# Where a soft threshold keeps its magnitudes: PSUM or SBUF, and two PSUM banks that change hands

## The chip, the core and the metric

The kernel runs on one core of a Trainium2 chip. TensorE (PE) multiplies, VectorE (DVE), ScalarE (ACT) and GpSimd (POOL) work element by element, and SyncE (SP) issues the transfers. Every engine runs its own instructions in the order of the program and waits on semaphores. Two memories lie beside the engines: SBUF, and PSUM, into which PE writes. PSUM is used here as eight banks; one bank holds 512 float32 numbers for each of the 128 partitions. The metric is the time of the program on the device in microseconds (us), and less is better.

## The reference

The input `x` is 4 images of 64 channels of 256 x 256 float32. Four layers follow each other:

```python
# layers 0, 2, 3: a 2-D convolution by FFT, zero padded to 512 x 512,
# with a separable filter per channel (hx, hy come out of two small networks)
k = jnp.einsum('ijk,imk->ijmk', hx, hy)[0]
y = irfft2(rfft2(x, s=(512, 512)) * rfft2(k) / 512)[..., :256, :256]
out = y + x * bias[:, None, None]
# layer 1: 2-D Haar transform, mixing of channels, soft threshold, inverse
f1 = haar2d(x)
for i in range(2):
    f4 = jnp.einsum('bchw,oc->bohw', f1 * v[i], conv_w[i])
    acc = acc + jnp.sign(f4) * jax.nn.relu(jnp.abs(f4) - tau[i])
y = haar2d(acc, inverse=True) + x
```

## The kernel before

All data are float32. The filter is separable, so a convolution is two products with Toeplitz matrices, rows and then columns. The images are taken in two **groups** of two images; each group goes through 32 rounds of two channels. The function `toeplitz` (L289) issues one block of a product: 16 products of 64 x 64 tiles with 256, 192, 128 and 64 columns, which the profile shows as 32 matmuls. `haar` (L302) issues a block of the Haar transform, 8 matmuls of 512 columns in the profile.

There are three phases, and each is a list of small pieces of program that `beside` (L929) lays among each other. The order on every engine is therefore written out by hand; no scheduler moves anything.

- Phase A (`phase_a`): layer 0 and the forward Haar transform, for both groups, into a DRAM tensor.
- Phase B (`phase_b(grp)`): the mixing of channels and the soft threshold. `phase_b(0)` lies beside the second half of phase A, and `phase_b(1)` beside the first half of phase C.
- Phase C (`phase_c`): the inverse Haar transform, then layers 2 and 3. For rounds t of group 0 it runs beside `phase_b(1)`; after that, from `beside(c[cut_c:], [], 0, 0)` on, it runs alone.

**Phase B.** It goes through 64 steps s of two units, u = 2s and u = 2s+1, one for each of the two sums over `i`. Of each unit:

- `mix` (L597): PE multiplies by `conv_w` into `f4`, a tile of two PSUM banks, of which there is one (`bufs=1`). 8 matmuls of 512 columns.
- `multiply` (L616, L622): DVE, `x = f4 * v`, from PSUM into SBUF. Two buffers.
- `sign` (L624, L628): ACT, `m = Sign(x)`, into SBUF. Three buffers.
- `magnitude` (L630, L634): ACT, `a = Abs(x)`, into `a`, a tile of two PSUM banks, one buffer.
- `less` (L636, L639): DVE, `a = a - tau`, in place.
- `threshold` (L641, L644): DVE, `m = max(a, 0) * m`, into SBUF.
- `add` (L652): POOL adds `m` and the old value into `g` (L659, L662, L663), and `store` (L666) issues the transfer to DRAM.

In the second group the odd units of steps 2 to 63 are **raw**: `multiply` only copies `f4` to SBUF (L619), and their threshold is done in phase C, when that runs alone (`shrink`, L761, with its operations at L778 to L787). So the second group has 66 units that take a magnitude (128 less 62 raw ones). Each of them brings one `less` and one `threshold`.

The pieces of `phase_b` are emitted in this order (L678): in piece j=0 of unit u come `multiply(u)`, `less(u-1)`, `add(u-2)`; in j=1 `mix(u+1)`, `sign(u)`, `threshold(u-1)`; in j=2 `magnitude(u)`. DVE therefore reads, step after step: multiply of 2s, copy of raw 2s+1, less of 2s, threshold of 2s, with the instructions of phase C between them.

**Phase C.** A round t has 18 pieces (L869): four blocks of rows of layer 2 (`c1r`), one of the inverse transform (`c0ps`), four of columns of layer 3 of round t-2 (`c2c`), four of rows of layer 3 of round t-1 (`c2r`), one `c0ps`, four of columns of layer 2 (`c1c`). Two blocks in a row share a pair of PSUM banks; a `c0ps` block has a pair of its own. A pair is emptied by two copies, which are emitted at the head of the next piece (`flush`): ACT copies `c1r`, `c2r` (L836) and `c0ps` (L824), and DVE adds the bias term to `c1c` and `c2c` (L855). POOL does the free part of the inverse transform (`ci`, L382), and its result is what `c0ps` multiplies.

**Who has which banks.** `banks` (L132) hands out pairs from a list of pools, `rings`, in turn. While phase C runs beside `phase_b(1)`, `rings` is `[acps]`, a pool of four banks, so two pairs take turns; the other four banks are `f4` and `a`. When phase C runs alone, `a` and `f4` are free: two banks become a third pair (`wide2`), and two hold the late threshold (`late_ps`).

```python
def banks(name):
    ring = rings[asked[0] % len(rings)]
    asked[0] += 1
    return [ring.tile([P, 2, N], F32, tag="ps", name=f"{name}_{r}") for r in range(2)]
```

Of the kernel before, what the change touches and what calls it, by code (L numbers as in the profile page):

```python
# [41 lines left out]
F32 = mybir.dt.float32  # L42
AF = mybir.ActivationFunctionType
ALU = mybir.AluOpType
PSUM = bass.MemoryType.PSUM
DRAM = bass.MemoryType.DRAM

P = 128
# [17 lines left out]
GROUPS = 2  # L66
NB = B // GROUPS
# [12 lines left out]
W = 2 * N  # L80
# [16 lines left out]
def conv_haar_kernel(  # L97
# [18 lines left out]
    def pool(name, bufs, stack=ctx, **kw):  # L116
        return stack.enter_context(tc.tile_pool(name=name, bufs=bufs, reuse_waits="tile", **kw))

    ac = pool("ac", 2)
    acps = pool("acps", 4, space=PSUM)  # L120
# [8 lines left out]
    rings = [acps]  # L129
# [391 lines left out]
    def phase_b(grp):  # L521
# [4 lines left out]
        def raw(u):  # L526
            return grp == GROUPS - 1 and u % 2 == 1 and FULL <= u // 2 < STEPS
        st = [dict() for _ in range(STEPS)]
        un = [dict() for _ in range(units)]
# [100 lines left out]
        def magnitude(u):  # L630
            if raw(u):
                return
            un[u]["a"] = bps.tile([P, NB, W], F32, tag="a", name=f"a_{grp}_{u}", bufs=1)
            nc.scalar.activation(un[u]["a"], un[u]["x"], AF.Abs)  # L634

        def less(u):  # L636
# [41 lines left out]
        def piece(u, j):  # L678
# [17 lines left out]
            elif j == 1:  # L696
                if u + 1 < units:
                    mix(u + 1)
                if u < units:
                    sign(u)  # L700
                if i and s < STEPS and grp == GROUPS - 1:
                    store_raw(s)
                if 0 < u <= units:
                    threshold(u - 1)
                if i == 0 and s > 0:

                    load_v(s + 2)
                    load_f(s + 3)
            else:
                if u < units:  # L710
                    magnitude(u)
                if i == 0 and s < STEPS:
                    exchange(s)
# [237 lines left out]
    bps = pool("bps", 2, during, space=PSUM)  # L951
# [3 lines left out]
    a, head = a[-2 * A_PIECES :], A_PIECES + BLOCKS  # L955
# [2 lines left out]
    beside(a_last, c_before[5:], 0, 5)  # L958
    during.close()
    bp = pool("b2", 2, during)  # L960
    bps = pool("bps2", 2, during, space=PSUM)

    mid = 3 * BLOCKS + 2
    main = c_first + a_end[:1] + c[:BLOCKS] + c[mid:C_PIECES] + a_end[1:] + c[BLOCKS:mid] + c[C_PIECES:cut_c]
    beside(main, phase_b(1), len(c_first) + len(a_end) + 2 * BLOCKS, 0)
    during.close()
    rings[:] = [acps, acps, pool("wide2", 2, space=PSUM)]
    late["sb"] = pool("late", 1)
    late["ps"] = pool("late_ps", 1, space=PSUM)
    beside(c[cut_c:], [], 0, 0)  # L970
# [119 lines left out]
```

## Time and profile before

| | |
|---|---|
| three runs | 2595.73, 2596.64, 2599.01 us; median 2596.64 |
| the profiled execution | 2597.8 us; its span 2595.7 us, so 2.1 us lie around the span |
| mean granted clock of TensorE | 0.979 |
| busy, share of the span | PE 2343.0 us (90%), DVE 1800.2 (69%), ACT 1325.6 (51%), POOL 2025.0 (78%) |
| moved by DMA | 685.25 MB, mean 264 GB/s |
| `phase_b(1)` beside phase C | first `multiply` at 1166.9 us, last `threshold` at 1880.8 us |

A row of the group view names line, engine, operation, output and inputs, the number of instructions, their busy time and mean duration, and the idle time of the engine before them with what ended it. In a timeline a row is: start in us, length in us, engine, line, operation, and in square brackets the time that the engine had waited and what released it. In a row of stretches the columns are the stretch, its length, and the busy time of PE, PEld (TensorE's weight loads), DVE, ACT and POOL, the granted clock, the busy share of the DMA engines and their GB/s.

### The profile page before, as it was taken

The page shows a single profiled execution, that of the slowest core. Times are in us where ns is not written, and L with a number is a line of the kernel's source. Part 1 is how long each engine was busy: PE and PEld are TensorE (multiplying, and loading weights), DVE is VectorE, ACT ScalarE, POOL GpSimd, SP SyncE. Part 2 cuts the span into 40 slices and gives each one's busy share as a digit, 9 for nine tenths or more (in the row PEclk, how much of TensorE's full clock was granted, in tenths as well). Part 3 has the DMA queues.
Part 4 walks back from the last instruction along what each step waited for, and adds up shares of the span by engine and source line. Part 5 has one row for each costly group of instructions (what it writes and reads, how often), then busy time and mean ns, then how long its engine had stood idle before and what let it go on. Part 6 is the DMA issues. An engine that isn't in the chain of part 4 may idle for free.

```text
span 2595.7 us, 118630 instructions
## 1 busy us (share of the span) xinstructions
PE 2343.0 (90%) x53292; PEld 1915.7 (74%) x53292; DVE 1800.2 (69%) x2049; ACT 1325.6 (51%) x2187; POOL 2025.0 (78%) x2428
## 2 busy tenths in 40 slices
PE   5999999788888888768999999999989999999999
PEld 4887877444444444547777877788889999999998
DVE  2555445799999999646666666666658777777773
ACT  1221112566666666226666665666655655655552
POOL 1898887899999999757657666766679999999991
PEclk8999999899999999979999999999999999999999
DMA  7676897699999999556989888888776666666653
GB/s 209 222 242 231 289 311 281 245 347 317 343 330 328 347 319 335 180 194 214 333 302 315 317 303 302 306 304 311 275 224 203 220 208 215 214 220 207 220 165 113
DMA packets 203678, 685.25 MB, mean 264 GB/s; under 512 B 29289, under 2 KB 30826, under 8 KB 190755
## 3 DMA queue, kind: packets, MB, share of 16 engines
q1 hardware_dynamic: 203171, 677.67, 75.8%
q8 instruction: 418, 6.85, 1.1%
q14 instruction: 89, 0.73, 0.1%
HBM read 427.93 MB, written 249.63 MB: 261 GB/s over the span
## 4 chain that ended last, share of the span: by engine, by line
PE 59%; DVE 13%; DMA 8%; POOL 8%; issue 5%; ACT 3%; SPq 2%; DVEq 0%; ACTq 0%; POOLq 0%
PE c2c L293 10%; PE c2r L293 9%; PE c1c L293 9%; PE c1r L293 9%; PE a1ps L293 6%; PE a2ps L293 5%; PE f L603 4%; PE c0ps L305 4%; DMA v<-in_v 3%; DVE x L622 3%; POOL fw L341 3%; POOL f L343 2%; DVE a L639 2%; DVE m L644 2%; PE a3ps L305 2%
## 5 line engine op out<-in xcount | busy, mean ns | idle before, releaser
L293 PEld LDWEIGHTS a2ps<-toep,ay 64*64 64x64 f32 x8192 | 313.2, 138 | 161.7 <-DVE f L474 85.0
L382 POOL TENSOR_TENSOR i<-i,g 128x16 f32<-128x16 f32 x744 | 398.3, 556 | 27.7 <-ACT g L359 0.6
L293 PE MATMUL a2ps<-toep,ay 64*64 64x128 f32 (+3 forms) x8192 | 360.1, 307 | 50.8 <-DVE f L474 42.4
L603 PE MATMUL f<-ft,mix 64*64 64x512 f32 x2048 | 312.0, 619 | 95.6 <-DVE x L622 80.2
L293 PEld LDWEIGHTS c2c<-toep,ch 64*64 64x64 f32 x8192 | 314.6, 134 | 59.0 <-ACT ch L836 25.9
L293 PEld LDWEIGHTS a1ps<-toep,x 64*64 64x64 f32 x8192 | 293.8, 134 | 83.8 <-issue 43.1
L293 PE MATMUL a1ps<-toep,x 64*64 64x64 f32 (+3 forms) x8192 | 338.8, 300 | 15.3 <-issue 12.3
L293 PEld LDWEIGHTS c1c<-toep,ch 64*64 64x64 f32 x8192 | 313.3, 134 | 51.6 <-ACT ch L836 26.6
L662 POOL TENSOR_TENSOR gt<-m,ft 128x512 f32<-128x512 f32 x128 | 163.6, 1278 | 236.3 <-DVE m L644 230.7
L293 PE MATMUL c1r<-toep,z 64*64 64x128 f32 (+3 forms) x8192 | 324.4, 299 | 21.5 <-issue 11.6
L293 PE MATMUL c2c<-toep,ch 64*64 64x192 f32 (+3 forms) x8192 | 328.7, 300 | 11.8 <-ACT ch L836 8.7
L293 PEld LDWEIGHTS c1r<-toep,z 64*64 64x64 f32 x8192 | 303.9, 134 | 46.6 <-issue 22.2
L293 PE MATMUL c1c<-toep,ch 64*64 64x128 f32 (+3 forms) x8192 | 324.3, 299 | 11.1 <-ACT ch L836 10.4
L382 POOL TENSOR_TENSOR ci<-i,g 128x1024 f32<-128x1024 f32 x124 | 318.2, 2586 | 4.5
L293 PE MATMUL c2r<-toep,cy 64*64 64x128 f32 (+3 forms) x8192 | 318.4, 298 | 2.9 <-issue 2.7
L293 PEld LDWEIGHTS c2r<-toep,cy 64*64 64x64 f32 x8192 | 301.4, 134 | 24.7 <-issue 13.3
L441 ACT COPY ay<-a1ps 128x512 f32<-128x512 f32 x256 | 137.4, 589 | 353.6 <-PE a1ps L293 353.0
L628 ACT ACTIVATE m<-x 128x1024 f32<-128x1024 f32 x194 | 206.3, 1063 | 194.2 <-DVE x L622 87.6
L639 DVE TENSOR_TENSOR a<-a,v 128x1024 f32<-128x1024 f32 x192 | 236.3, 1231 | 49.0 <-ACT a L634 48.9
L836 ACT COPY ch<-c2r 128x512 f32<-128x512 f32 x256 | 137.5, 591 | 247.1 <-PE c2r L293 246.6
L634 ACT ACTIVATE a<-x 128x1024 f32<-128x1024 f32 x194 | 199.6, 1029 | 109.4 <-DVE m L644 109.4
L855 DVE SCALAR_TENSOR_TENSOR cy<-z,bias_sb,c1c 128x512 f32<-128x512 f32 x256 | 176.9, 742 | 109.5 <-PE c1c L293 109.5
(80 smaller groups left out, 3869.2 us busy)
## 6 DMA issues: line engine op xcount, KB each, us to landing
toep<-filt SPq DMA_DIRECT2D x384, 224.0 KB, 5.3
ft<-coef SPq DMA_DIRECT2D x128, 512.0 KB, 7.4
v<-in_v SPq DMA_DIRECT2D x64, 1024.0 KB, 9.4
mixed<-gt SPq DMA_DIRECT2D x128, 512.0 KB, 7.5
g<-mixed SPq DMA_DIRECT2D x256, 256.0 KB, 5.7
x<-in_x SPq DMA_DIRECT2D x128, 256.0 KB, 4.7
coef<-f SPq DMA_DIRECT2D x128, 256.0 KB, 4.2
x<-in_x SPq DMA_DIRECT2D x32, 1024.0 KB, 7.8
```

The lines of the kernel that those rows point to most:

```text
L293: nc.tensor.matmul(ps[r][half(c), j % 2, k * ROW :], data[half(r), c, k, bass.ts(j, ROW)], t(r, c)[:, : N - k * ROW], start=k == 0, stop=k ...
L305: nc.tensor.matmul(ps[r][half(c)].rearrange("p h k -> p (h k)"), matrix[half(r)], pairs(r, c).rearrange("p h k -> p (h k)"), start=True, s ...
L341: nc.gpsimd.tensor_tensor(diffs, even, odd, ALU.subtract)
L382: engine.tensor_tensor(to, s, d, op)
L441: later(lambda y=y, ps=ps: nc.scalar.copy(y, ps))
L603: nc.tensor.matmul(un[u]["f4"][half(q), b, :], mixers[0][half(r), bass.ts(i, C)], st[s]["f"][half(r), b], start=True, stop=True, tile_posi ...
L628: nc.scalar.activation(un[u]["m"], un[u]["x"], AF.Sign)
L634: nc.scalar.activation(un[u]["a"], un[u]["x"], AF.Abs)
L639: nc.vector.tensor_tensor(un[u]["a"], un[u]["a"], both(u, "tau"), ALU.subtract)
L662: nc.gpsimd.tensor_tensor(g[:, 0], m[:, 0], st[s]["f"][:, 0], ALU.add)
L836: later(lambda y=y, ps=ps: nc.scalar.copy(y, ps))
L855: nc.vector.scalar_tensor_tensor(to, of, bias_sb[:, at : at + 1], ps, ALU.mult, ALU.add)
```

## The change

In the second group `magnitude` no longer takes the PSUM tile `a`: it writes |x| over `x` in SBUF, and `less` and `threshold` work from there. The two banks that `a` had are handed to `rings` as a third pair already while phase C runs beside `phase_b(1)`, and not only when it runs alone. The first group keeps `a` in PSUM.

```diff
         def magnitude(u):
             if raw(u):
                 return
-            un[u]["a"] = bps.tile([P, NB, W], F32, tag="a", name=f"a_{grp}_{u}", bufs=1)
+            if grp == GROUPS - 1:
+                un[u]["a"] = un[u]["x"]
+            else:
+                un[u]["a"] = bps.tile([P, NB, W], F32, tag="a", name=f"a_{grp}_{u}", bufs=1)
             nc.scalar.activation(un[u]["a"], un[u]["x"], AF.Abs)
...
     bp = pool("b2", 2, during)
+    rings[:] = [acps, acps, pool("wide2", 2, space=PSUM)]
     bps = pool("bps2", 2, during, space=PSUM)
...
     during.close()
-    rings[:] = [acps, acps, pool("wide2", 2, space=PSUM)]
     late["sb"] = pool("late", 1)
```

The instructions of every engine and their order are the same before and after; only the places of the operands and the waits differ. Because three lines are added, lines from 634 on carry a number three higher in the profile after (four higher between the two places of `rings`).

## Prediction

> **What bounds the kernel now.** I read the busy time by stretches first: phase C beside `phase_b(1)` (1170 to 1890 us), and phase C alone (1960 to 2500).
>
> ```profile
> 1170.00:1890.00 720.00, 677.89 (x15469) 567.18 (x15465) 453.67 (x477) 448.06 (x786) 482.14 (x571) 1.00 0.85 298
> 1960.00:2500.00 540.00, 539.26 (x14729) 512.86 (x14725) 417.65 (x446) 315.45 (x587) 504.57 (x504) 1.00 0.66 213
> ```
>
> PE leads in both. Alone, it is full; beside the mixing it has gaps, while DVE, ACT and POOL are idle a third of the time. To size the gaps I put the matmuls of the timeline in order of start. Where nothing holds PE, a Toeplitz block of 32 matmuls starts 1.09 us after the one before, a block of 8 (`f`, `c0ps`) takes 0.86 us. From the first to the last whole block of the first stretch 719.5 us pass, and its blocks at these paces make 633.1: PE stalls for 86.4 us. Alone, with three pairs of banks, it is 5.7 us of 537.8.
>
> Then I asked what ended each of the stalls over 0.1 us: the DVE or ACT instruction that ended within 0.15 us before PE went on. Three kinds come out.
>
> (1) **Bank stalls**, 18.5 us. The block needs a pair of banks whose emptying copy has just ended (0.05 us before); 21 blocks, 14.8 us, and in 17 of them the second half waits 0.2 us more for the second copy, 3.7 us. Nearly all are the block behind a `c0ps`: `c0ps` takes only 0.86 us, and the pair used before it is wanted again. The waits of the weight loads name them, and the timeline shows one.
>
> ```profile
> PEld c1c L293 <- ACT ch L836: 19.4, 29, 2.1
> PEld c2c L293 <- ACT ch L836: 16.9, 31, 1.9
> ```
>
> ```profile
> 1520.36 1.07 PE L305 MATMUL c0ps<-ci,inverse_sb 64*64 64x512 f32 x6
> ...
> 1520.51 1.25 ACT L650 COPY other<-ft 64x512 f32<-64x512 f32 x2
> ...
> 1521.78 1.07 ACT L836 COPY ch<-c2r 128x512 f32<-128x512 f32 x2
> ...
> 1522.42 2.66 PE L293 MATMUL c1c<-toep,ch 64*64 64x256 f32 x58 [0.99 <-ACT ch L836]
> ```
>
> ACT was at `other` when `c2r` was done; the first of the two copies (0.6 us each) ended at 1522.37, and PE went on at 1522.42.
>
> (2) **Stalls at the mixing**, 17.3 us in 21 places: `mix(u+1)` needs the only `f4`, and DVE has not read unit u out of it. Below, DVE must add `o` first, which PE itself releases, and `multiply` ends at 1310.39.
>
> ```profile
> 1307.85 1.41 DVE L855 SCALAR_TENSOR_TENSOR o<-cy,bias_sb,c2c 128x512 f32<-128x512 f32 x2 [1.00 <-PE c2c L293]
> ...
> 1309.17 1.22 DVE L622 TENSOR_TENSOR x<-f,v 128x1024 f32<-128x1024 f32 x1
> ...
> 1310.53 1.09 PE L603 MATMUL f<-ft,mix 64*64 64x512 f32 x8 [0.48 <-DVE x L622]
> ```
>
> (3) The rest, some 50 us: no data wait ends it ("issue"), or `ci` was late once (5.5 us at 1219).
>
> **The change, part by part.** The order of instructions is the same on every engine, and so are all transfers and SP's queue. Four things differ.
>
> *A third pair.* A pair is now wanted again three calls later, so a block that shares banks with the second last call finds them empty one pair earlier: at least 0.86 us, mostly 2.2. The largest single bank stall was 1.4 us. Phase C alone shows the rotation of three: 5.7 us of stalls although DVE is at 77% there. I take all of kind (1): **-18.5 us**. Bounds: 0 (each is replaced by a later stall), and -18.5 less a tenth of kind (3), -23, if unnamed stalls hide some more.
>
> *`Abs` writes SBUF.* 66 instructions. Into PSUM they took 1038 ns in this stretch, and `Sign`, SBUF to SBUF, 1068: 66 x 30 ns = 2.0 us on ACT. It also waits for its own engine's `Sign`, which reads what it overwrites; the nearest row is DVE's gap of 0.05 us between `less` and `threshold`, so 3 us more. ACT idles 272 us of the stretch, and the copies behind it now have a spare pair: 0 on the path. Without that cover it would be 5 us.
>
> *`a` is gone, `x` lives longer.* `Abs` no longer waits for the threshold of the unit before; that was 1.8 us in the stretch, on ACT: 0. Each of the two buffers of `x` is held until `threshold`, but is wanted again only by the `multiply` two steps (22 us) later, on the same engine: 0.
>
> *`less` and `threshold` have two SBUF inputs*, 132 instructions on DVE. Now one comes from PSUM, and they take 1226 and 1223 ns, always. The only DVE line beside a busy POOL that reads two SBUF tensors of this size is the late threshold's first, L778; the lines after it read one from PSUM.
>
> ```profile
> L778 DVE TENSOR_TENSOR x<-raw,rows x64: 1226/1754/3422, 1903.0 to 2513.6; 128x1024 f32<-128x1024 f32 x64
> L784 DVE TENSOR_TENSOR x<-x,rows x64: 1222/1223/1233, 1909.3 to 2518.1; 128x1024 f32<-128x1024 f32 x64
> ```
>
> L778 is not slow; it waits. All 64 durations are 1226 ns plus what POOL's instruction, where that had begun first, still had to go, less 0.14 us. It holds the other way too:
>
> ```profile
> 2154.72 5.80 POOL L803 TENSOR_TENSOR g<-g,shrunk 128x1024 f32<-128x1024 f32 x2 [0.44 <-ACT g L359]
> ...
> 2157.08 1.23 DVE L778 TENSOR_TENSOR x<-raw,rows 128x1024 f32<-128x1024 f32 x1
> ```
>
> The second of these two POOL additions took 3.4 us in place of 2.37: it stood behind DVE's 1.23. [...]
>
> So 0 where POOL is idle, and a wait where it is not. Had the 132 instructions met POOL where they start in this trace, 29 of 66 `less` and 19 of 66 `threshold` would find it busy, and wait 39.3 us in all. A `threshold` right behind a `less` that had to wait meets POOL's next instruction as well, which was held meanwhile: 13 times, 14.1 us more. DVE gets 39 to 53 us of work, and idles 266. What of it reaches PE? Late copies of `c1c`, `c2c`: the third pair takes them, as in phase C alone. A late `multiply` holds `mix`: I carried the 39.3 us forward along DVE's row, let its idle times take what they can up to the next `multiply`, and 17.7 us are left there; PE's own slack between that and `mix` leaves 10.8 us, in 11 places. For a `threshold` the lock is shown by no row (all two-SBUF SCALAR_TENSOR_TENSOR of this size run with POOL idle); below, it is free, above, as `less`. I take it as locked, by the nearest row, L778. I take **+10.8 us**; bounds 0 (no lock) and 31.8 (17.7 + 14.1, no slack).
>
> POOL, too, is held: 27 of its instructions start inside a `less` or `threshold` of this trace, 18.9 us in all. It idles 224 us for `m`, and `ci` is ready 2.8 to 19 us ahead of `c0ps` in all rounds but one (t=4): 0.
>
> Sum: 18.5 - 10.8 = 7.7 us less. PE is the chain from here to the end (539.26 of 540 alone), so the end comes that much earlier: 2597.8 - 7.7 = 2590.1 for the profiled execution, which lies 1.2 us above the median of the runs: **2589 us**.
>
> **Rivals.** About 0.2% (5 us) is what a measurement of this kernel can tell from no change.
>
> - *The port lock costs more than the banks gave*: slower. Place: `mix`, behind a `multiply` that a locked `less` or `threshold` made late; kind (2) grows. For it: one `f4`, and DVE goes from 63% to 70% of the stretch. Against it: POOL mostly waits for `m` while `threshold` runs (47 of 66 find it idle). It decides once over 18.5 of the 53.4 us, 35%, reach PE; my share is 10.8 of 39.3, 27%. At one half, 26.7 - 18.5 = +8: 2605. At its bound, 31.8 - 18.5 = +13: 2610. Chance 0.28.
> - *Banks give, mixing takes*: a PE that is earlier meets the same `multiply` and the same late instructions (kind 3, at a DMA share of 0.85). If 15% of the gain goes there and the loss grows with 53.4/39.3 to 14.7: 15.7 - 14.7 = 1 us less, 2596. Chance 0.27.
> - *No lock here*: L778 writes PSUM, `less` does not. Then all 18.5 us: 2578. Against it: the wait of L778 fits POOL's inputs, not its output. Chance 0.10.
> - *The pairs don't rotate*, or `wide2` waits for phase B's old banks: the first group's last `threshold` starts at 1060.8, and DVE writes round 0's `ci`, which the first `c0ps` needs, only at 1094: nothing speaks for it. With the lock alone it would be the first rival.
>
> **Numbers.** My forecast has 0.35. Faster by over 0.2%: 0.35 + 0.10 = 0.45; within: 0.27; slower: 0.28. The range goes from no lock with some more hidden bank stalls, 2576, to the bound of the first rival, 2610.
>
> **What would show it.** Stalls of `c1c` and `c2c` behind `c0ps` gone from PE's waits. `less` (L642) and `threshold` (L647) with a minimum of 1223 to 1226 ns and a mean of 1.5 to 1.8 us, their excess equal to POOL's rest; POOL's `gt` and `ci` with maxima near 3.5 us. PE's stretch of `phase_b(1)` about 8 us shorter, with stalls at `mix` up from 17 to 28 us. I am wrong if the stalls at `mix` grow by more than the bank stalls shrink, or if `threshold` never exceeds 1.23 us. [...]

## The result and the profile after

The changed kernel takes 2596.61 us (median of 20 runs, 2583.64 to 2604.18); beside it the kernel before takes 2598.99 us (20 runs, 2592.25 to 2609.35). The ratio is 0.9985, with a 95% interval of 0.9972 to 0.9998: some 4 us less, between 0.5 and 7. The forecast was 7.7 us less. The profiled execution took 2595.18 us, its span is 2591.5 us.

The stretches of the profile after, with the columns as before:

```profile
1170.00:1890.00 720.00, 666.42 (x15670) 550.87 (x15665) 505.83 (x479) 453.77 (x788) 534.35 (x584) 0.99 0.86 300
1960.00:2500.00 540.00, 538.29 (x14591) 510.56 (x14584) 423.62 (x445) 311.25 (x576) 497.45 (x492) 1.00 0.66 212
```

Beside the mixing DVE and POOL are each busy 52 us more, with nearly the same number of instructions. Most of that is waiting inside them (worked out below). PE shows a larger count of matmuls in the same 720 us, so it got further.

The waits of PE and its weight loads in that stretch (waited for: us in total, times, longest us), after:

```profile
PE f L603 <- DVE x L622: 18.3, 17, 2.4
...
PE c0ps L305 <- POOL ci L382: 10.0, 1, 10.0
...
PEld c1c L293 <- ACT ch L839: 2.5, 7, 1.0
...
PEld c2c L293 <- ACT ch L839: 0.2, 1, 0.2
```

and two of the same rows before:

```profile
PE c0ps L305 <- POOL ci L382: 5.1, 1, 5.1
...
PE f L603 <- DVE x L622: 3.6, 8, 0.5
```

The waits for the banks' copies are all but gone (19.4 us for `c1c` and 16.9 for `c2c` before). The wait of `mix` for `multiply` has grown, and so has one single wait for `ci`. POOL reaches that `ci` later; its instructions before, then after:

```profile
1194.15 2.40 POOL L382 TENSOR_TENSOR i<-i,g 128x128 f32<-128x128 f32 x4
...
1214.74 4.66 POOL L382 TENSOR_TENSOR ci<-i,g 128x1024 f32<-128x1024 f32 x2
```

```profile
1197.10 4.37 POOL L382 TENSOR_TENSOR i<-i,g 128x128 f32<-128x128 f32 x4
...
1220.32 4.64 POOL L382 TENSOR_TENSOR ci<-i,g 128x1024 f32<-128x1024 f32 x2
```

The `ci` pair takes as long as before but starts 5.6 us later, behind instructions of POOL that were held.

The instructions that moved to SBUF, as groups (busy us, mean ns | idle time before them), two rows before and two after:

```profile
L644 DVE SCALAR_TENSOR_TENSOR m<-a,m 128x1024 f32<-128x1024 f32 x65 | 79.5, 1223 | 5.0
L639 DVE TENSOR_TENSOR a<-a,v 128x1024 f32<-128x1024 f32 x64 | 78.5, 1226 | 16.1 <-ACT a L634 16.0
```

```profile
L647 DVE SCALAR_TENSOR_TENSOR m<-x,m 128x1024 f32<-128x1024 f32 x66 | 107.5, 1629 | 5.0
L642 DVE TENSOR_TENSOR x<-x,v 128x1024 f32<-128x1024 f32 x64 | 101.2, 1581 | 18.5 <-ACT x L637 18.4
```

Both means rose. With the two first units, whose tau lies in `raw`, `less` carries (1593 - 1226) x 66 = 24 us of waiting, `threshold` (1629 - 1223) x 66 = 27 us. It is waiting for POOL: 130 of the 132 durations are, within 0.03 us, 1222 ns plus what the instruction then running on POOL still had to go, less 0.14 us. One place shows how this reaches PE:

```profile
1394.22 5.70 POOL L382 TENSOR_TENSOR ci<-i,g 128x1024 f32<-128x1024 f32 x2
1394.31 3.37 DVE L642 TENSOR_TENSOR x<-x,v 128x1024 f32<-128x1024 f32 x1
...
1397.79 3.21 DVE L647 SCALAR_TENSOR_TENSOR m<-x,m 128x1024 f32<-128x1024 f32 x1
1400.92 1.40 DVE L858 SCALAR_TENSOR_TENSOR cy<-z,bias_sb,c1c 128x512 f32<-128x512 f32 x2
...
1402.24 1.21 DVE L622 TENSOR_TENSOR x<-f,v 128x1024 f32<-128x1024 f32 x1
...
1403.60 1.09 PE L603 MATMUL f<-ft,mix 64*64 64x512 f32 x8 [2.26 <-DVE x L622]
```

`less` starts 0.09 us after POOL's first `ci` and takes 3.37 us instead of 1.23; POOL's second `ci` is held meanwhile, and `threshold`, right behind `less`, waits for it: 3.21 us. The two copies `cy` and `multiply` follow late, and `mix` waits 2.26 us.

**The stalls by kind.** I took every run's profile through the same account as the one of before: the stretch from one block at the start of `phase_b(1)` to one at its end, the same two in every kernel, 633.9 us at PE's own pace, and the stalls over it. The rest of kind (3) needed a closer look. In the trace the packets of DMA queue 8 are all of 16,384 bytes:

```profile
q8 instruction: 418, 6.85, 1.1%
```

PE executes 53,292 matmuls and as many weight loads; 106,584 over 418 is 255 for one packet. So I take these packets for PE's code, one **code block** of about 255 instructions each. In PE's order of instructions, the pauses without a wait stand one such block apart, and each ends 1.2 to 1.6 us (median 1.4) after a packet has landed. Four in a row, from the run early_after below:

```
packet (us)           PE goes on at   at its instruction   distance
1249.24 to 1250.31    1251.57         40903
1255.23 to 1256.34    1257.70         41157                254
1261.30 to 1262.36    1263.69         41411                254
1267.63 to 1268.77    1270.37         41665                254
```

Kind (3) is therefore split: **code** is a stall that is neither bank nor mix and in whose block PE goes on 1.20 to 1.65 us after a packet of its code (by chance one in twelve would: the window is 0.45 us wide, and packets come every 5.7 us); **ci** is the late `c0ps` of t=4, at 1217 to 1232; the rest is unnamed. All in us, one profile each; ratios are of the times, with their 95% intervals. The times of one kernel scatter by some 5 us (standard deviation of 20 runs of before, and of after), so a difference of a few us between two rows is not shown by them alone.

| kernel | ratio to before | stretch | bank | mix | code | ci | rest |
|---|---|---|---|---|---|---|---|
| before | | 722.2 | 18.5 | 17.3 | 30.8 | 5.5 | 16.1 |
| after | 0.9985 (0.9972 to 0.9998) | 714.2 | 0.6 | 30.7 | 26.4 | 10.3 | 12.2 |
| lock_only | 1.0017 (1.0001 to 1.0033) | 728.6 | 29.7 | 19.0 | 18.0 | 7.8 | 20.3 |
| f4_two | 1.0010 (0.9994 to 1.0026) | 719.7 | 39.5 | 0.8 | 19.0 | 6.6 | 19.9 |
| early_before | 0.9971 (0.9957 to 0.9986) | 713.8 | 18.0 | 0 | 41.2 | 6.6 | 14.1 |
| early_after | 0.9953 (0.9934 to 0.9971) | 709.0 | 0 | 11.4 | 42.0 | 10.3 | 11.4 |
| nopool_before | 1.0009 (0.9994 to 1.0023) | 725.3 | 26.9 | 15.1 | 31.1 | 0 | 18.3 |
| nopool_after | 0.9970 (0.9954 to 0.9986) | 711.7 | 5.6 | 14.5 | 45.6 | 0 | 12.0 |
| nov_before | 0.9912 (0.9895 to 0.9930) | 697.4 | 23.4 | 19.3 | 3.1 | 5.5 | 12.3 |
| nov_after | 0.9903 (0.9883 to 0.9922) | 689.8 | 0.5 | 36.3 | 3.4 | 8.6 | 7.1 |
| nov_early_after | 0.9845 (0.9825 to 0.9865) | 673.9 | 0.4 | 13.1 | 9.7 | 10.3 | 6.5 |
| spread_after | 0.9984 (0.9973 to 0.9995) | 717.0 | 0.4 | 28.0 | 32.9 | 10.3 | 11.5 |
| early_spread_after | 0.9964 (0.9948 to 0.9981) | 710.5 | 0.9 | 13.5 | 43.0 | 10.3 | 8.9 |
| early_spread_before | 0.9967 (0.9948 to 0.9985) | 710.8 | 18.2 | 0.1 | 37.7 | 6.7 | 14.1 |

For the change itself: bank -17.9, mix +13.4, ci +4.8, code -4.4, rest -3.9, together -8.0 us in the stretch.

### The profile page after: what moved, and what is told of

Same layout as the page of the kernel before. It is cut to its first block, busy times and chain, and to the rows that moved or that the text cites. A ratio compares the mean times of both kernels' runs of the same rounds, so it can differ in the third digit from the quotient of the medians.

```text
span 2591.5 us, 118522 instructions
## 1 busy us (share of the span) xinstructions
PE 2324.7 (90%) x53292; PEld 1892.3 (73%) x53292; DVE 1858.3 (72%) x2049; ACT 1329.6 (51%) x2187; POOL 2067.0 (80%) x2428
## 4 chain that ended last, share of the span: by engine, by line
PE 53%; DVE 17%; POOL 9%; DMA 9%; issue 6%; ACT 3%; SPq 1%; DVEq 0%; ACTq 0%; POOLq 0%
PE c2c L293 9%; PE c2r L293 9%; PE c1r L293 8%; PE c1c L293 7%; PE a1ps L293 6%; PE a2ps L293 5%; PE f L603 4%; PE c0ps L305 3%; DVE m L647 3%; DVE x L622 3%; DMA v<-in_v 3%; POOL fw L341 2%; DVE a L642 2%; POOL f L343 2%; PE a3ps L305 2%
## 5 line engine op out<-in xcount | busy, mean ns | idle before, releaser
L382 POOL TENSOR_TENSOR i<-i,g 128x16 f32<-128x16 f32 x744 | 411.9, 574 | 27.7 <-ACT g L359 0.6
L603 PE MATMUL f<-ft,mix 64*64 64x512 f32 x2048 | 297.6, 619 | 109.5 <-DVE x L622 96.7
L293 PE MATMUL a1ps<-toep,x 64*64 64x128 f32 (+3 forms) x8192 | 339.0, 300 | 18.6 <-DMA x<-in_x 13.8
L382 POOL TENSOR_TENSOR ci<-i,g 128x1024 f32<-128x1024 f32 x124 | 336.3, 2732 | 4.6
L293 PE MATMUL c1r<-toep,z 64*64 64x256 f32 (+3 forms) x8192 | 320.4, 300 | 19.2 <-ACT z L827 10.8
L293 PE MATMUL c2c<-toep,ch 64*64 64x128 f32 (+3 forms) x8192 | 320.7, 299 | 9.6 <-ACT ch L839 6.5
L293 PE MATMUL c1c<-toep,ch 64*64 64x192 f32 (+3 forms) x8192 | 316.9, 298 | 9.3 <-ACT ch L839 7.0
L474 DVE TENSOR_TENSOR f<-a3ps,wrow_sb 128x512 f32<-128x512 f32 x256 | 161.3, 682 | 132.6 <-PE a3ps L305 132.6
L622 DVE TENSOR_TENSOR x<-f,v 128x1024 f32<-128x1024 f32 x192 | 233.4, 1216 | 21.2 <-PE f L603 20.4
L839 ACT COPY ch<-c1r 128x512 f32<-128x512 f32 x256 | 137.8, 593 | 205.4 <-PE c1r L293 205.0
```

The costliest lines, as they stand in the source:

```text
L293: nc.tensor.matmul(ps[r][half(c), j % 2, k * ROW :], data[half(r), c, k, bass.ts(j, ROW)], t(r, c)[:, : N - k * ROW], start=k == 0, stop=k ...
L382: engine.tensor_tensor(to, s, d, op)
L474: later(lambda f=f, ps=ps, w=w: nc.vector.tensor_tensor(f, ps, w, ALU.mult))
L603: nc.tensor.matmul(un[u]["f4"][half(q), b, :], mixers[0][half(r), bass.ts(i, C)], st[s]["f"][half(r), b], start=True, stop=True, tile_posi ...
L622: nc.vector.tensor_tensor(un[u]["x"], un[u]["f4"], both(u, "v"), ALU.mult)
L839: later(lambda y=y, ps=ps: nc.scalar.copy(y, ps))
```

## The experiments

**Theory 1** is that of the forecast: the third pair gave 18 us, and the lock took some 13 back at `mix`. By the lock, or the port lock, only this is meant: of a DVE instruction with two SBUF operands and one of POOL's, one waits while the other runs (in the profile before, L778 took up to 3.42 us instead of 1.23, and POOL's L803 up to 3.49 instead of 2.37). Where in the hardware they meet, no run shows. **Theory 2** is the rival: the lock is hidden, and stalls removed in one place simply appear in the next, since PE comes earlier to the same late thing.

### One half alone: lock_only

The third pair is handed out as late as before.

```diff
     bp = pool("b2", 2, during)
-    rings[:] = [acps, acps, pool("wide2", 2, space=PSUM)]
...
     during.close()
+    rings[:] = [acps, acps, pool("wide2", 2, space=PSUM)]
     late["sb"] = pool("late", 1)
```

> Only the magnitudes in SBUF; the third pair of banks comes as late as before, so two banks stand empty beside phase_b(1). Theory 1 (the port lock costs about 13 us at mix, and the third pair gave 18 us): the stalls at mix go from 17.3 us to 27 to 31 us, the bank stalls stay at 18.5 us or grow by some us, because o is copied later; the stretch of phase_b(1) is 10 to 20 us longer than before, and the time is 10 to 20 us over before (ratio 1.004 to 1.008). Theory 2 (the lock is hidden in DVE's idle time; the stalls at mix grew in the changed kernel only because PE, no longer held at the banks, comes earlier to the same multiply): stalls at mix stay at 17 to 20 us, time within 3 us of before (ratio 0.999 to 1.001).

Measured: 2605.81 us against 2599.29, 6.4 us more in the stretch. Slower, as theory 1 has it, but by less than its 10 to 20 us, and in another place: mix 19.0, which is the number of theory 2, and bank 29.7, more than theory 1 had. With two pairs the late DVE shows first where its own copies empty the banks; this row of the weight loads' waits stands high, and has no match among the large rows of before:

```profile
PEld c1r L293 <- DVE cy L858: 14.3, 24, 1.9
```

The code stalls fell by 13 us. That PE's code catches up while PE stands at a bank would explain it, but is not shown: f4_two below fits (bank 39.5, code 19.0), nopool_before does not (bank 26.9, code 31.1). The lock has a price, and where it is paid depends on which buffer is scarce.

### The two banks put to another use: f4_two

As lock_only, and `f4` of the second group has two buffers.

```diff
-            un[u]["f4"] = bps.tile([P, NB, W], F32, tag="f4", name=f"f4_{grp}_{u}", bufs=1)
+            un[u]["f4"] = bps.tile([P, NB, W], F32, tag="f4", name=f"f4_{grp}_{u}", bufs=1 + grp)
```

> Magnitudes in SBUF as in the change, but the two banks that come free are a second f4 of the second group; the inverse stage keeps two pairs. mix no longer waits for the multiply of the unit before. If the stalls at mix are DVE's lateness at the single f4: they go to 0 to 3 us, also with the port lock; the bank stalls (18.5 us before) stay or grow to some 22 us. Theory 1: time 10 to 17 us under before (ratio 0.9935 to 0.996), better than the change itself (0.9985). Theory 2 expects the same 17 us from the stalls at mix, but lets PE, earlier at the banks, lose most of it again: bank stalls over 28 us and a time within 6 us of before.

Measured: no faster (1.0010). Mix fell to 0.8 as both theories had it; bank rose to 39.5, which is theory 2. Against lock_only, which lacks nothing but the second `f4`, mix fell by 18.2 us and the stretch by 8.9: two pairs of banks took back about half of what the mixing no longer held up.

### The multiply one piece earlier: early_before and early_after

```diff
-                if u < units:
+                if u < units and (grp < GROUPS - 1 or u == 0):
                     multiply(u)
...
             else:
+                if grp == GROUPS - 1 and u + 1 < units:
+                    multiply(u + 1)
                 if u < units:
                     magnitude(u)
```

> The kernel before, with multiply(u+1) of the second group one piece earlier on DVE (behind the pieces of mix(u+1), ahead of the residual copies that the next piece flushes). If the stalls at mix come from multiply being queued behind those copies, they go from 17.3 us to under 5 us; the bank stalls of 18.5 us stay, or rise to 22 us where the copies o now stand behind the multiply. Theory 1: time 8 to 16 us under before (0.994 to 0.997). Theory 2 (a gain of one kind is taken back by the other): bank stalls up to 30 us, time within 5 us.

Measured: 2591.87 us, 7.4 us less, the edge of theory 1's range. Mix is 0, so it is the copies ahead of `multiply` on DVE that make it late. Bank did not grow, against theory 2; but 10.4 us came back as code stalls, which neither had named.

> The changed kernel with the same earlier multiply. With three pairs a late residual copy costs nothing, and an early multiply frees f4. Theory 1: stalls at mix from 30.7 us to under 10 us (what is left is the lock itself holding the multiply, which reads f4 in PSUM and one SBUF tensor, or POOL), bank stalls stay under 2 us; time 20 to 30 us under before (ratio 0.989 to 0.992), 16 to 26 us under the change. Theory 2: stalls at mix fall as well, but the other stalls (47 us now) grow by half of it, and the time is 10 to 15 us under before (0.994 to 0.996).

Measured: 2588.20 us, 11.1 us less than before: theory 2's number. Mix fell to 11.4, bank is 0, and code rose by 15.6 us. These are PE's own pauses (first row of before, then three of early_after):

```profile
PE c1r L293 <- issue: 11.3, 11, 2.6
```

```profile
PE c1r L293 <- issue: 15.6, 17, 1.7
PE c2r L293 <- issue: 6.4, 7, 1.7
PE c1c L293 <- issue: 3.7, 5, 2.0
```

### Is it the lock? nopool_before and nopool_after

The same edit in the kernel before and in the changed one:

```diff
                 s["ops"] = inverse_free(s["g"], s["ci"], f"i{t}_", nc.vector if t < 2 else nc.gpsimd)
+                if 2 <= t < alone:
+                    s["ops"] = blank(s["ci"])
+
+        def blank(dst):
+            nc.gpsimd.memset(dst, 0.0)
+            yield
```

> The kernel before, with POOL's part of the inverse transform (rounds 2 to 31) replaced by one memset of its result, so that part is not computed; POOL has only the additions of phase_b left beside it. Without a two-SBUF instruction on DVE in this stretch the lock plays no part: time within 6 us of before, some of it gained where ci was late once (5.5 us at 1219).

> The changed kernel with the same part left out: less and threshold now rarely meet a busy POOL, and their mean falls from 1.23 us to 1.21 to 1.25 us with maxima rare. Theory 1 (the port lock is what brings the stalls at mix from 17 to 31 us): stalls at mix within 3 us of those of the kernel before with the same part left out, and the difference in time between the two grows from 3 to 4 us to 10 to 16 us. Theory 2 (the stalls at mix grew because PE arrives earlier): they grow here too, by 8 us or more, and the difference stays at 3 to 8 us.

Measured: 2600.25 and 2591.18 us, 9.1 us apart. With POOL's transform left out the instructions on two SBUF operands are nearly as short as they were with one in PSUM (means of 1223 and 1226 ns); nopool_after:

```profile
L647 DVE SCALAR_TENSOR_TENSOR m<-x,m 128x1024 f32<-128x1024 f32 x66 | 82.8, 1254 | 5.0
L642 DVE TENSOR_TENSOR x<-x,v 128x1024 f32<-128x1024 f32 x64 | 78.9, 1233 | 25.2 <-ACT x L637 25.0
```

and the stalls at mix do not grow: 15.1 and 14.5. So the 13 us at mix are the lock, as theory 1 says. One objection is left: in nopool_after the code held PE for longer, and a PE that is late for that reason waits less at mix. The trace of the changed kernel answers it without leaving anything out. I followed DVE's order back from each late `multiply`, up to the last gap in which DVE was idle. By this coarser count (27.2 us at mix after, 12.3 before), 12 of the 24 stalls stand behind a `less` or `threshold` that waited for POOL, and these waits cover up to 16 us; the stalls with no such wait ahead of them come to 8.8 us, no more than before. PE's earlier arrival is not needed to explain the growth. In early_after ten of the eleven stalls left at mix are of the first kind. Yet the two are only 13.6 us apart in the stretch and not the 21 that the banks gave: code rose from 31.1 to 45.6. Theory 2 is right in this form. (The 5.6 us at a bank in nopool_after are one single late copy.)

### Is it the code, and why is it late? nov_before and nov_after

61 loads of 512 KB are left out; the instructions of PE, DVE, ACT and POOL stay.

```diff
             d = st[s]
+            if grp == GROUPS - 1 and s > 2:
+                d["v"], d["tau"] = kept
+                return
             d["v"], d["tau"] = [], []
+            if s == 2:
+                kept[:] = [d["v"], d["tau"]]
```

> The kernel before, but the second group loads v and tau only for steps 0 to 2 and uses those of step 2 for steps 3 to 63 (so it computes with the wrong factors there); 61 transfers of 512 KB are gone from the stretch of phase_b(1), all instructions of the engines stay. Theory C (a stall that no data wait ends is PE waiting for its own code: it ends some 1.4 us after a 16 KB packet of the instruction queue has landed, and 17 such stalls, 16 us, stand in the stretch of the kernel before; the code comes late because the DMA engines are 0.85 busy): DMA share falls to about 0.74, these stalls fall to under 5 us, the bank stalls and the stalls at mix stay or grow by a few us, the time is 8 to 14 us under before (0.9945 to 0.997). Theory D (they are not code, but TensorE's own pauses): they stay at 14 to 18 us and the time is within 3 us of before.

> The changed kernel with the same loads left out. Theory C: with the code on time nothing takes back what the third pair gives, apart from the port lock at mix: code stalls from 19 to 25 us in 25 places to under 5 us, time 18 to 25 us under before (0.990 to 0.993), so 8 to 12 us under the kernel before with the same loads left out, against 3 to 4 us with them. Theory D: code stalls stay, and the difference between the two stays at 3 to 4 us.

Measured: 2575.80 and 2572.56 us. The stretch of nov_after, its DMA share (last but one column) at 0.76, where the row of the changed kernel above has 0.86:

```profile
1170.00:1850.00 680.00, 642.05 (x15250) 514.43 (x15246) 504.33 (x473) 448.68 (x778) 531.68 (x564) 0.99 0.76 266
```

Code stalls fall from 30.8 to 3.1 and from 26.4 to 3.4 us: theory C, and by more than it expected, because it had counted only the pauses without a wait (16 us before, where the account above has 30.8); many stand at the head of a block of matmuls, where a wait that was already over hides them. The second half of the expectation failed. The two kernels are 7.6 us apart in the stretch, hardly less than the 8.0 with the loads, and 3.2 us in the medians: bank gives 22.9 us between these two and mix takes 17.0, where it took 13.4 with the loads.

The intervals show where the time goes. I placed the borders of the code blocks by these pauses (254.2 to 254.5 instructions apart) and looked when the next packet starts after PE has entered a block. By these figures the next block can begin no sooner than this start, plus the packet (1.0 us), plus 1.4 us.

```
                       start of next packet after PE enters a block   blocks that need over 5.2 us
                       median     90%
before, stretch        2.6 us     4.2 us                               48%
nov_before, stretch    1.6        2.9                                  13%
before, alone          1.3        2.2                                   3%
```

The middle row is the least certain, as nov_before has few pauses to place borders by; with the borders of before, whose instructions on PE are the same, it reads 1.9 us and 24%. The order of the rows does not depend on it.

PE needs 633.9 us for some 122 blocks of the stretch, 5.2 us for one. Beside the mixing every second block of code is at its limit; alone it is one in thirty. That the packet starts later because the DMA engines are busy fits the shares (0.85, 0.76 and 0.66), and leaving the loads out moved it; what holds the packet inside the queues no run shows. The code costs PE little here at a DMA share of 0.66 (alone, where all stalls together are 5.7 us of 537.8) and at 0.76 with the loads left out (3 us of stalls); at 0.85, beside the mixing, it costs 31 us.

### Both removed: nov_early_after

The edits of nov_after and early_after together.

> The changed kernel with the second group's loads of v and tau left out for steps 3 to 63 (those of step 2 are used, so it computes with the wrong factors there), and with multiply(u+1) one piece earlier: code on time and f4 free early. Theory C (with the early multiply, PE's code took back what the mixing gave: 42 us of code stalls against 26): code stalls 3 to 6 us, stalls at mix 36 to about 11 us, the stretch of phase_b(1) 668 to 675 us instead of 690, time 2550 to 2558 us (0.982 to 0.985). Rival (the early multiply is itself late by the lock): stalls at mix stay over 25 us, time 2565 us or more (0.988).

Measured: 2552.42 us and a stretch of 673.9, in theory C's range. Code is 9.7, a little over it, mix 13.1. With the loads in place, the early multiply was worth 5.2 us of the stretch (714.2 to 709.0); with the code on time it is worth 15.9 (689.8 to 673.9).

### Bursts or sum: spread_after, early_spread_after, early_spread_before

```diff
                 if i == 0 and s > 0:
-
-                    load_v(s + 2)
+                    if grp < GROUPS - 1:
+                        load_v(s + 2)
                     load_f(s + 3)
+                if i and s > 0 and grp == GROUPS - 1:
+                    load_v(s + 2)
```

> The changed kernel with the load of v and tau (512 KB) issued one unit later than the load of ft (512 KB), and not right ahead of it; the same transfers in all. If it is the bursts of transfers that make PE's code late: code stalls from 26 us to 15 to 20 us, time 4 to 9 us under the change (0.995 to 0.997 of before). If it is the sum of what is moved (DMA share 0.86 in the stretch): code stalls stay at 24 to 30 us and the time stays within 3 us of the change (0.9975 to 0.9995).

> The changed kernel with the early multiply and the later load of v and tau: a whole kernel that may beat both. If bursts count: code stalls 42 to 25 to 32 us, time 2575 to 2582 us (0.992 to 0.995); if the sum counts: as with the early multiply alone, 2586 to 2590 us (0.995 to 0.9965).

> The kernel before (magnitudes in PSUM, two pairs of banks in the stretch) with the same two edits. It tells what the change itself is worth once the mixing waits no more: with early multiply alone the two stood at 0.9971 and 0.9953, 3.7 us apart. Expected 3 to 6 us over the run with the change (2580 to 2592 us, 0.994 to 0.998); if the lock's price has gone with the early multiply, up to 10 us.

Measured: 0.9984 with code at 32.9 us, 0.9964 with 43.0, and 0.9967 with 37.7. Moving a load by one unit helps nothing. That speaks for the sum of what is moved and against bursts of this kind; no other move was tried. Between early_spread_before and early_spread_after the change itself is worth nothing that the runs can tell: with `multiply` early, PSUM with two pairs and SBUF with three take the same time (stretches 710.8 and 710.5).

The best kernel is early_after: 0.9953 of before, and 8.4 us by the medians under the change. That it beats early_before (0.9971) is not sure, as the intervals overlap.

## Why the prediction was half right

- *A third pair, -18.5 us*: right, 18.5 to 0.6 us in the stretch. Nothing else stepped in at the banks.
- *Abs to SBUF, 0*: right. It takes a mean of 1065 instead of 1038 ns in the stretch, 1.8 us on ACT for the 66. `less` waits for it a little longer (20.8 us in all, 18.6 before), and no wait of PE names it but 0.7 us of its weight loads.
- *less and threshold, +10.8 us*: the mechanism was right, `threshold` included; the size was a little low. DVE waited 51 us: the term took the 39.3 us of the first meetings alone, and the waits of a `threshold` behind a late `less` (14.1 us in the forecast) came as well. 13.4 us reached `mix` instead of 10.8, a share of 26% (27%). nopool_after and the waits ahead of the late `multiply` show that it is the lock. The shortest durations are 1206 and 1211 ns, where the forecast had 1223 to 1226. One reading of the forecast is too broad: what it says of L778 holds for 45 of its 64 durations. In 17 cases the record of POOL's instruction begins 8 to 38 ns earlier and yet it is POOL that is held, and in two DVE came 9 ns before POOL's end and waited for POOL's next instruction.
- *POOL held, 0*: this step failed. POOL's busy time from 1166 to 1880 us rose by 50 us, from 490 to 541 (durations summed), where 18.9 were expected; 44 us of it are longer durations, the rest is six instructions more in that time. The cover of 2.8 to 19 us ahead of `c0ps` holds in all rounds but t=4, which had been late already: its `ci` is now 10.3 us late instead of 5.5. These 4.8 us stand in every run with the three pairs and POOL at work, except that nov_after has 3.1.
- *Kind (3), taken as a constant*: the step that the account lacked. Some 60% of it (30.8 us) is PE waiting for its own code. It is no constant: it gave 4.4 us here, and took 10 to 16 us back in the two runs with the early `multiply`. The upper bound of 23 us for the third pair reckoned with it in one direction alone.
- *The sum, -7.7 us*: the stretch became 8.0 us shorter, so the sum came out, but in part by luck: misses of single terms made up for each other (ci +4.8, mix +2.6 and bank +0.6 against code -4.4 and the rest -3.9). *The end comes that much earlier* did not come out in full: span -4.2 us, ratio 0.9985. In these two profiles all of the gap is in the stage that runs alone, which takes 699.9 us before and 704.4 after for the same blocks. Over all 14 profiles this stage takes 699.4 to 706.1 us, also among kernels that are the same there (699.9 and 703.1 us for before and early_before); the seven kernels with the third pair in the stretch average 703.5, the seven others 702.2. So I take it for chance; what makes the stage vary is not shown. Whether the runs' gap between 8 and 4 us is more than this spread stays open: the interval reaches to 7.3 us.
- *The rivals*: the measured time, some 4 us less, is within 0.2% of before as "banks give, mixing takes" had it, but not by its sum: the loss at mix was 13.4, not 14.7, and the gain at the banks was hardly less (17.9 us). "No lock" is excluded by L647 and L642, "the pairs don't rotate" by the bank stalls.

## What to carry to other kernels

Before you remove a stall, ask what the engine would wait for next, and count in its own code: find the instruction queue's packets, how many instructions each holds, and how long the engine takes for them. PE had 5.2 us of work in a block here, and beside the mixing 48% of the blocks needed longer for the next one to come. Where that is so, a freed buffer may gain little: the two banks gained 0.15%, and fewer bytes on the DMA engines 0.9% (61 loads of 512 KB left out). And the operand moved from PSUM to SBUF cost DVE nothing here only where POOL was idle (from 1206 and 1211 ns there, means of 1593 and 1629 ns beside POOL's transform): look for the other engine's instructions beside yours, and for what stands behind both.

## What the runs showed of the hardware

- PE's code came in packets of 16,384 bytes, about 255 instructions. PE went on 1.2 to 1.6 us after a packet's end, and the next packet started 1.3 us after PE entered a block at a DMA share of 0.66, 2.6 us at 0.85 (medians). Stalls of that kind: 31 us of 722 (3 us with 61 loads left out).
- The SCALAR_TENSOR_TENSOR with two SBUF operands waited for POOL as the TENSOR_TENSOR did (L647: 1211 to 3215 ns, L642: 1206 to 3374; with POOL's transform left out, means of 1254 and 1233). Both engines waited: DVE 51 us, and POOL's durations grew by 44 us.
- Two such instructions one behind the other each met an instruction of POOL, 3.37 and 3.21 us instead of 1.23.
